# First GNN layer: one PSUM bank for small results in two halves, and a block's end with three steps between its hops

## The chip, the cores and the metric

The kernel runs on one core of a Trainium2 chip. The metric is device time in microseconds. The kernel before has a median of 3425.99 us over three runs (3420.14 to 3426.87).

A core has five engines that run their own instruction streams and wait for each other by semaphores: TensorE (PE: matrix products and transposes, with PEld its weight loads), VectorE (DVE), ScalarE (ACT), GpSimd (POOL, which here issues the gathers) and SyncE (SP, which issues DMAs; ScalarE issues some too). TensorE writes to PSUM, and VectorE or ScalarE read the results from there.

## The reference, cut to what matters

The whole computes two rounds of a graph layer and an expert layer on 6250 nodes of 256 values. The change is in the first graph layer:

```python
def _L0_gnn_ref(x, edge_index, edge_attr, u, batch, W1, b1, W2, b2):
    row, col = (edge_index[0], edge_index[1])
    h = jnp.concatenate([x[row], edge_attr], axis=1)
    h = jax.nn.relu(h @ W1 + b1)
    agg = jax.ops.segment_sum(h, col, num_segments=N_NODES)
    cnt = jax.ops.segment_sum(jnp.ones((h.shape[0],), h.dtype), col, num_segments=N_NODES)
    agg = agg / jnp.maximum(cnt, 1.0)[:, None]
    out = jnp.concatenate([x, agg], axis=1)
    return jax.nn.relu(out @ W2 + b2)
...
x = x + _L0_gnn_ref(_layernorm(x, axis=-1), edge_index, edge_attr_256, ...)
x = x + _L0_ffn_ref(_layernorm(x, axis=-1)[None], ...)[0]
```

There are 106250 edges, sorted by their destination `col`. The expert layer that follows begins with a normalization of x and a product with W_gat; both are already made here, at the end of each block of nodes.

## The kernel before, in words

**Tiling.** The nodes lie in 49 windows of 128 (a block's end, in the change's words, is a window's end). The edges of a window are worked on in three groups, so there are 147 groups, numbered q. A group has six tiles of 128 edges.

**One group.** `load_sources` gathers the rows of the sources (six indirect DMAs by POOL) into one of four ring buffers h. `load_attr` loads the edges' attributes in eight DMAs, four issued by SyncE and four by ScalarE (L1410). `turn` transposes them on VectorE (L1500). `hidden(q, j)` multiplies two of the six tiles by the lower half of W1 into PSUM (ph, L1115, 8 records in the trace each time). `join` adds the gathered rows on VectorE (L1518), and a relu follows on ScalarE (L1519). `add_up` sums the edges of equal destination on TensorE, by matrices of zeros and ones that `equal` made (pe, L1541).

**The order.** It is written out by hand: `Ordered.pin` keeps each engine's instructions in program order through the main loop (L1632 to L1656). An iteration q has join(q-1), hidden(q, 0), add_up(q-2), the gathers of q+2, turn(q+1), hidden(q, 2), equal(q), hidden(q, 4), and at last new attribute loads. Generators are advanced at three places between, by `steps`. This text calls them slots:

- A, between hidden(q, 0) and add_up: a step of the sorting for a later stage (VectorE), then one step of each window's end that is under way;
- B, between hidden(q, 2) and hidden(q, 4): one step of each window's end;
- C, after hidden(q, 4): a step of `windows` (which prepares the indices of later windows), then one step of each window's end.

**A window's end** (`end_of`, L1547) starts after its last add_up, in slot B. It is a chain of hops between engines: divide by the count (ag, ScalarE L1554); transpose (TensorE L1109, into pt) and copy out (gt, ScalarE L1110); four products with W2 (pm, L1115, a pt tile too); bias, relu, residual and statistics of x on VectorE (L1566 to L1575) and a square root on ScalarE (L1576); the normalized x (xn, ScalarE L1582); transpose and copy out to b_all (the same lines); two products with the W_gat columns (pg, L1115, pt again), and three copies on ScalarE (L1593 to L1595). A `yield` ends a step. With A1 for slot A of the group after the one in which the end started, the steps lie at B0, A1, C1, A2, B2, A3, C3, ten steps in all. One group has three, and a window ends every nine steps.

**The PSUM tile pt.** [...] one buffer of one bank, for everything that is small. A pt tile is 128 x 256 float32[...]. The next tile of the pool waits until the last one has been read. Besides a window's end, `find_starts` (L1034) and `load_windows` (L1152) use it in slot C, for six blocks of seven windows each, during the first 100 groups; and `sorted_edges` (L1332) at the end of the layer.

**The window loads.** `load_windows` also lets SyncE issue 14 small loads, raw_src and raw_dst (L1146), once per block. ScalarE's attribute loads [...] wait for those before them.

## Time and profile before

The profile is of one execution, which took 4171.77 us; its span, from the first to the last instruction, is 4169.9 us. The runs without a profile took 3426 us. So a duration taken from the profile is compared with the profile's own total.

| row of the page | busy us | mean ns |
|---|---|---|
| ph<-w1b,et, TensorE, x3528 | 869.1 | 399 |
| pe<-h,eq, TensorE, x3168 | 256.9 | 397 |
| h<-y_dram,src, POOL gathers, x882 | 850.7 | 965 |
| h<-ph,h, VectorE join, x147 | 258.2 | 1756 |
| h<-h, ScalarE relu, x147 | 218.2 | 1484 |
| et<-ea, VectorE turn, x147 | 260.8 | 1774 |

| small work of the windows' ends (trace, in the first layer) | mean ns |
|---|---|
| pt<-ident,o (transpose, 2 records of a kind each time) | 287 |
| pt<-w,b_all and pt<-w,o (pm, 8 records) | 391, 400 |
| pt<-wgx,b_all (pg, 4 records) | 260 |
| o<-pt and b_all<-pt, ScalarE copies | 368 |
| o<-pt,b; x_all<-o,x_all; ln_st<-x_all, VectorE | 417, 425, 427 |
| o<-x_all,off,ln_rs, ScalarE | 600 |

How to read it: a line of the page names line, engine, operation, what is written and read, and how often; then busy time, the mean of one, and the idle time of the engine just before, with what ended it. TensorE's records overlap, so the mean of one is longer than what one adds. A float32 product is two records. The granted TensorE clock was 0.856 of full speed over the span, and 0.93 in the first layer.

### The profile page before, as it was taken

Reading aid. Unit: us, or ns where it says so; the run is one execution under the profiler, and the core shown is the slowest. Engines: PE = TensorE matmul, PEld = TensorE weight load, DVE = VectorE, ACT = ScalarE, POOL = GpSimd, SP = SyncE. Lnnn points to the kernel's source line nnn. Section 1 sums busy time; section 2 is a strip of 40 time slices with the busy share of each in tenths; the row PEclk is TensorE's granted clock in tenths of the full one; section 3 lists DMA queues with packets and bytes.
Section 4 is the critical chain, followed back from the end, with each engine's and each line's share of the span. In section 5 each row is a group of like instructions: output and inputs, shape, how many; then the busy total and the mean of one; then the engine's idle time right before and its main releaser. Section 6 shows DMA issues by size and latency. Waiting matters only on the chain.

```text
span 4169.9 us, 57220 instructions
## 1 busy us (share of the span) xinstructions
PE 3317.5 (80%) x18509; PEld 2590.9 (62%) x18509; DVE 2154.3 (52%) x5685; ACT 1125.4 (27%) x2014; POOL 2256.1 (54%) x2364
## 2 busy tenths in 40 slices
PE   7787889888889985888898888785356766867788
PEld 5566666666666664677787777673234544555566
DVE  5565666665555653656455657564223333433344
ACT  4122222222222222324435344452011211111123
POOL 0555566566666635455454545524666666665651
PEclk8899999999999997999999999896567777776678
DMA  6676767777777732323333334233111111111110
GB/s 192 156 166 152 169 160 173 170 166 165 171 168 176 167 99 54 78 66 95 82 84 99 92 88 114 73 79 96 45 45 52 50 50 50 51 51 48 52 49 21
DMA packets 698912, 428.56 MB, mean 103 GB/s; under 512 B 531272, under 2 KB 640315, under 8 KB 698604
## 3 DMA queue, kind: packets, MB, share of 16 engines
q0 software_dynamic: 89408, 178.08, 18.3%
q1 hardware_dynamic: 365948, 187.21, 16.9%
q10 hardware_dynamic: 243248, 59.52, 7.2%
q8 instruction: 150, 2.46, 0.3%
q14 instruction: 158, 1.29, 0.1%
HBM read 382.05 MB, written 42.49 MB: 102 GB/s over the span
## 4 chain that ended last, share of the span: by engine, by line
PE 47%; another core or an unknown queue 10%; issue 10%; DVE 7%; POOL 5%; ACT 3%; DMA 2%; SPq 1%; DVEq 0%; ACTq 0%; POOLq 0%
PE ph L1115 21%; PE py L1115 10%; PE pe L2524 4%; POOL hg L1128 4%; PE pt L1115 3%; PE po L1884 3%; PE pe L1541 3%; POOL h L1128 1%; PE pa L1821 1%; DMA rb<-low_dram 1%; PE pt L1109 1%; ACT hh L1720 1%; ACT L1720 1%; DVE eq L2503 1%
## 5 line engine op out<-in xcount | busy, mean ns | idle before, releaser
L1128 POOL DMA_INDIRECT h<-y_dram,src x882 | 850.7, 965 | 645.5 <-issue 511.0
L1128 POOL DMA_INDIRECT hg<-hp_dram,src x831 | 786.9, 947 | 460.9 <-issue 230.8
L1128 POOL DMA_INDIRECT sg<-gat_dram,src x640 | 613.4, 958 | 613.3 <-DVE px L1856 334.0
L1115 PE MATMUL ph<-w1b,et 128*128 128x256 f32 x3528 | 869.1, 399 | 28.6 <-issue 22.1
L1115 PEld LDWEIGHTS ph<-w1b,et 128*128 128x128 f32 x3528 | 681.9, 198 | 196.8 <-issue 104.9
L2524 PE MATMUL pe<-eq,hg 128*128 128x96 f32 (+15 forms) x2036 | 376.5, 334 | 150.6 <-issue 90.4
L2524 PEld LDWEIGHTS pe<-eq,hg 128*128 128x128 f32 x2036 | 361.3, 252 | 214.6 <-issue 147.9
L1115 PE MATMUL py<-w,hh 128*128 128x256 f32 x1568 | 415.3, 404 | 77.2 <-ACT hh L1720 34.6
L1518 DVE TENSOR_TENSOR h<-ph,h 128x1536 f32<-128x1536 f32 x147 | 258.2, 1756 | 371.7 <-remote 164.3
L1519 ACT ACTIVATE h<-h 128x1536 f32<-128x1536 f32 x147 | 218.2, 1484 | 762.5 <-DMA ea<-in_edge_attr_dram 284.1
L2503 DVE TENSOR_SCALAR eq<-px,dst,ew 128x96 f32<-128x96 f32 x831 | 261.4, 367 | 312.2 <-remote 117.1
L1115 PE MATMUL ph<-b_all,w 128*128 128x256 f32 (+1 forms) x1600 | 411.4, 397 | 10.5 <-issue 10.3
L1115 PEld LDWEIGHTS py<-w,hh 128*128 128x128 f32 x1568 | 302.4, 201 | 130.3 <-ACT hh L1720 40.8
L1115 PEld LDWEIGHTS ph<-b_all,w 128*128 128x128 f32 x1600 | 304.6, 200 | 53.5 <-issue 16.5
L1541 PE MATMUL pe<-h,eq 128*32 128x257 f32 x3168 | 256.9, 397 | 68.1 <-issue 63.2
L1884 PE MATMUL po<-pp,B 128*128 128x240 f32 (+10 forms) x1280 | 261.8, 345 | 10.2 <-issue 8.4
L1500 DVE STREAM_TRANSPOSE et<-ea 128x1536 f32<-128x1536 f32 x147 | 260.8, 1774 | 14.8 <-issue 7.8
L1720 ACT ACTIVATE hh<-ph,b 128x256 f32<-128x256 f32 (+1 forms) x400 | 165.5, 467 | 360.9 <-remote 127.2
L1884 PEld LDWEIGHTS po<-pp,B 128*128 128x128 f32 x1280 | 222.3, 195 | 25.0 <-issue 9.7
L1541 PEld LDWEIGHTS pe<-h,eq 128*32 128x32 f32 x3168 | 104.1, 112 | 177.6 <-issue 124.9
L1115 PE MATMUL py<-ew,g 65*128 65x256 f32 x392 | 140.7, 485 | 49.8 <-DVE x_all L2479 33.5
L1863 DVE TENSOR_TENSOR pp<-px,A 128x960 f32<-128x960 f32 (+10 forms) x160 | 156.0, 975 | 42.1 <-remote 26.0
(339 smaller groups left out, 3825.0 us busy)
## 6 DMA issues: line engine op xcount, KB each, us to landing
ea<-in_edge_attr_dram SPq DMA_DIRECT2D x588, 96.0 KB
ea<-in_edge_attr_dram ACTq DMA_DIRECT2D x588, 96.0 KB
y<-y SPq DMA_DIRECT2D x196, 128.0 KB
w<-in_L_ffn_W_dram SPq DMA_DIRECT2D x48, 512.0 KB
y<-ys SPq DMA_DIRECT2D x96, 256.0 KB
rb<-low_dram SPq DMA_DIRECT2D x80, 256.0 KB
h<-y_dram,src POOLq DMA_INDIRECT x882
hg<-hp_dram,src POOLq DMA_INDIRECT x831
```

The source lines that it names most:

```text
L1109: TE.transpose(pt[:, c, :], src[:, c * P : (c + 1) * P], ident)
L1115: TE.matmul(dst, lhs(c), rhs(c), start=c == 0, stop=c == n - 1)
L1128: GP.indirect_dma_start(out=dst, out_offset=None, in_=table[0:NP, :], in_offset=IndirectOffsetOnAxis(ap=idx, axis=0),)
L1500: V.transpose(et[q].rearrange("p c m k -> p m c k"), ahead.pop(q).rearrange("p i m (c k) -> p (i m) c k", c=2),)
L1518: V.tensor_add(h, ph.pop(q), h)
L1519: SC.activation(h, h, AF.Relu)
L1541: TE.matmul(sums[w][b * Q : (b + 1) * Q, :], eq[k][:, j, at], h[:, i * NT + j, 0:WS], start=g == 0 and j == NT - 1, stop=g == last_of[b] a ...
L1720: SC.activation(hidden[u][:, f, :n, :], ph[:, f - f0, :n, :], AF.Gelu, bias=b1[:, e, f : f + 1],)
L1863: V.tensor_tensor(pps[g, half][:, :, 0:n, :], pay[:, js, :].unsqueeze(2).to_broadcast([P, HG, n, HV]), near[g][:, js, 0:n].unsqueeze(3).to ...
L1884: TE.matmul(po.rearrange("p b v -> p (b v)"), B[:, j, :], pp[:, j, 0:n, :].rearrange("p b v -> p (b v)"), start=half == 0 and j == 0, stop ...
L2503: V.tensor_scalar(equals[k][:, j, :], lanes[:, 0:NW], dst_of[:, t : t + 1], ew[:, t : t + 1], op0=OP.is_equal, op1=OP.mult,)
L2524: TE.matmul(sums[b][:, lo - t0 * P : hi - t0 * P], hg[:, j, :], eq[:, j, lo - n0 : hi - n0], start=False, stop=after >= (t0 + n) * P,)
```

## The change

A class `Halves` takes the whole bank as one tile and hands out its two halves in turn. In `end_of` four places that had two yields get three, so that a window's end has fourteen steps, and the steps lie at B0, B1, B2, C2, A3, A4, A5. Ends of two windows then overlap by five steps instead of one. In `sorted_edges` the tile's shape is cut to what a half holds.

```diff
+class Halves:
+
+    def __init__(self, pool, width):
+        self.width, self.last = width, 1
+        self.bank = pool.tile([P, 2, width], F32, name="pt")
+
+    def tile(self, shape, dtype, name):
+        n = math.prod(shape[1:])
+        assert dtype == F32 and n <= 2 * self.width
+        if n > self.width:
+            v = self.bank.rearrange("p a k -> p (a k)")[:, 0:n]
+        else:
+            self.last = 1 - self.last
+            v = self.bank[:, self.last, 0:n]
+        return v if len(shape) == 2 else v.rearrange("p (c k) -> p c k", c=shape[1])
...
-                pt = pst.tile([P, 4, P], F32, name="pt")
+                pt = pst.tile([P, 2, P], F32, name="pt")
...
-                tc.tile_pool(name="p1", bufs=1, space=PSUM) as psm,
+                tc.tile_pool(name="p1", bufs=1, space=PSUM) as pends,
...
+                psm = Halves(pends, D)
...
                     SC.activation(ag, pe[:, 0:D], AF.Copy, scale=rc)
-                    yield
-                    yield
+                    for _ in range(3):
+                        yield
                     gt = wk.tile([P, D], F32, name="o")
                     transposed(psm, gt, ag)
-                    yield
-                    yield
+                    for _ in range(3):
+                        yield
                     pm = psm.tile([P, D], F32, name="pt")
...
                     SC.activation(xn, x_all[:, w, :], AF.Identity, bias=off, scale=rs)
-                    yield
-                    yield
+                    for _ in range(3):
+                        yield
                     transposed(psm, b_all[:, w, :], xn)
-                    yield
-                    yield
+                    for _ in range(3):
+                        yield
                     pg = psm.tile([P, D], F32, name="pt")
```

More of the change, by code (lines that the diff above doesn't have):

```diff
@@ L1 @@
+import math
 from contextlib import ExitStack
```

## The prediction

> **What bounds the kernel now.** I read the page first, for the share of each engine and its slices.

> ```profile
> span 4169.9 us, 57220 instructions
> ...
> PE 3317.5 (80%) x18509; PEld 2590.9 (62%) x18509; DVE 2154.3 (52%) x5685; ACT 1125.4 (27%) x2014; POOL 2256.1 (54%) x2364
> ```

> Then the table of stretches, for the first layer alone (joins run from 107.7 to 1512.8 us):

> ```profile
> 150.00:1000.00 850.00, 736.08 (x4534) 549.48 (x4533) 525.98 (x1024) 191.87 (x321) 507.34 (x528) 0.93 0.74 165
> 1000.00:1500.00 500.00, 448.51 (x2736) 332.54 (x2736) 285.18 (x478) 116.34 (x196) 308.95 (x318) 0.93 0.73 166
> ```

> The first column of times is the stretch, then PE, PEld, DVE, ACT, POOL busy. PE is at 87% and 90%, no other engine over 62%. So the layer is TensorE's, and only what TensorE waits for counts. Third, TensorE's order of time over one whole window of three groups:

> ```profile
> 1309.17 0.38 PE L1109 MATMUL pt<-ident,o 128*128 128x128 f32 x2
> 1309.48 1.51 PE L1541 MATMUL pe<-h,eq 128*32 128x257 f32 x24
> 1310.92 3.72 PE L1115 MATMUL ph<-w1b,et 128*128 128x256 f32 x16
> 1314.47 1.03 PE L1115 MATMUL pt<-w,b_all 128*128 128x256 f32 x4
> 1315.34 1.03 PE L1115 MATMUL pt<-w,o 128*128 128x256 f32 x4
> 1316.20 1.89 PE L1115 MATMUL ph<-w1b,et 128*128 128x256 f32 x8
> ...
> 1332.21 0.38 PE L1109 MATMUL pt<-ident,o 128*128 128x128 f32 x2
> ```

> From one first transpose (1309.17) to the next (1332.21) it is 23.04 us without a gap: nothing to win here. POOL's 18 gathers, 0.95 us each and 0.30 between, need 22.5 us in the same time, so it is next in line. Last, what TensorE waited for in the earlier stretch, where the window loads run beside:

> ```profile
> PE pt L1115 <- DVE dst L1170: 20.9, 3, 10.5
> ...
> PE pt L1109 <- DVE ix_g L1164: 10.6, 2, 10.3
> PE pt L1115 <- DVE start L1036: 10.4, 2, 10.0
> PE pt L1115 <- ACT h L1519: 5.2, 3, 4.1
> ...
> PE pt L1115 <- ACT b_all L1110: 2.9, 1, 2.9
> ```

> The columns are us in all, times, longest. All rows with pt add up to 73 us. But four waits of about 10 us (41 us) lie where DVE, ACT and PE all stand and only POOL goes on. Such holes come about every 56 us also where no pt is near (DVE idle 10.83 us before 1357.83), so these four are not pt's to give back. Some 32 us are left: (a) pm or pg behind VectorE's reading of a window tile in the same slot C: 0.4 to 2.3 us, six clean ones, mean 0.8; (b) the first transpose behind the readers of the last pg: 4.0, 2.0, 2.0, 0.5, 0.3, together 8.8; (c) ScalarE held up by the loads of raw_src and raw_dst: 4.1, 3.9, 2.9, 1.3, 1.2, 0.8, together 14.2; (d) others, 1.9.

> **Part 1, the halves.** They add no instruction. What they allow depends on whether a write to one half may run while the other is read. No trace shows it, since the pool had one buffer, whose next tile always waited for the last reader. [...] The built program has it so: a first transpose into one half waits for the ScalarE copy out of the other, and pm for the three pg copies. By address, every wait of kinds a to d would go (9 + 8.8 + 14.2 + 1.9, less 3 for VectorE below): -31 us. By bank the hand-overs stay, and their distance decides. I take the bank. What the halves do give is that pm may lie unread while a window tile uses the other half.

> **Part 2, the steps.** With a group's slots A, B, C, a window ends thus, before: B0 ag, A1 first transpose, C1 pm, A2 normalize, B2 xn, A3 second transpose, C3 pg. After: B0, B1, B2, C2, A3, A4, A5. The same instructions run; the order changes.

> *Gone.* C holds no pm or pg any more. Of 18 uses of pt by windows (6 blocks, 3 each) 11 stood before a pm or pg by their group numbers, at 0.8: -9 us. The first transpose no longer follows pg by one slot: -8.8. Kind d: -1.9. Together **-20 us**. What is late next is POOL, 0.55 us a window behind, 27 us over 49 windows, so this gain would fit.

> *New: two hand-overs one slot apart.* Second transpose (A4) and the next window's first (B4) share a group; so do pg (A5) and the next pm (B5). Within a group join starts some 0.2 us after the first matmul, 1.76, then ScalarE's relu 1.48: it ends at 3.5, or near 4.1 where the four ea issues (2.2 us) come first. The copy (0.37) is done at 4.5; slot B comes at 1.8 + 0.3 + 1.4 + 1.8 = 5.3. So 0.8 us of slack, and about as much for pg's three copies (0.5). Before, the same copies had until C, 1.8 us more. No cost in a quiet window. Where relu is late, it is paid. Of the groups with that transpose, eleven had a relu later than that by 0.1 to 2.8 us without window loads, 8 us together; of those with pm's B, about 1: **+9 us**.

> *The window loads.* Six times the four ea issues on ScalarE wait for loads that SyncE spreads over 10 us, and relu stands behind them (ScalarE's order of time, then TensorE's):

> ```profile
> 740.51 1.48 ACT L1519 ACTIVATE h<-h 128x1536 f32<-128x1536 f32 x1 [3.63 <-DMA h<-y_dram,src]
> ...
> 748.09 5.01 ACTq L1410 DMA_DIRECT2D ea<-in_edge_attr_dram  x4
> 753.38 1.48 ACT L1519 ACTIVATE h<-h 128x1536 f32<-128x1536 f32 x1 [11.11 <-DMA ea<-in_edge_attr_dram]
> ```

> ```profile
> 756.11 0.44 PE L1109 MATMUL pt<-ident,o 128*128 128x128 f32 x2 [1.33 <-issue]
> ```

> The group begins at 746.08 and its relu ends at 754.86, 8.8 later; TensorE paid only 1.33, at the next transpose. After, pm (1.73) leaves the C before this group and stands in its B: the relu ends at 10.5 by the group's own start, the copies at 11.0, slot B is at 5.6: a wait of 5.4. The same for the others, by group: q9 5.3, q24 2.7, q38 8.4, q52 none (its B holds nothing), q80 6.4. Sum 28 against 14.2: **+14 us**. Those of q38 and q80 overlap a hole and may be smaller.

> *VectorE at C2.* Normalize (0.42, 0.42, 0.43, 0.18, 0.15, with gaps 1.74) moves from A2 to C2, ahead of join and its PSUM buffer. pm ends one pair of hidden (1.8 us) before the group does, so the chain is hidden by that pair. Where a window tile is read at C2 too (7 times) the pair is used up; join is then 2.7 us late, the transpose of the group after it 0.4: **+3 us**. Without the pair it would be 1.7 x 49 = 85 us.

> *ScalarE and its queue.* The Sqrt comes before the four ea issues of that group, which start about 3 us later; they are needed three groups (23 us) on. Costs nothing; uncovered, 3 us a window. SyncE's and POOL's queues are not passed. The write of gat_dram comes a few slots later, once in seven windows, with no reader before the layer ends. At the end of the layer the last window takes the same chain, with six more expert matmuls (0.43 each) before its pg and one reload of ScalarE's table (1.28) fewer: bounds -2 to +3. I take **+2**, since TensorE is nearer to being the bound there (gaps of 0.4 to 1.3 us from 1527 to 1546) than ScalarE.

> **Sum**: -20 + 9 + 14 + 3 + 2 = +8, by the profiled execution 4171.8 + 8 = 4180 (its span 4169.9 and 1.9 around it). The runs shown have a median of 3425.99, 18% less. The holes, 10 us in 56, have the same share, but no run shows that they are missing there. I carry the 8 us over whole: **3434 us**, +0.23%.

> **Rivals.**
> 1. *The gain is left alone.* Relu's lateness is partly the holes' doing; without them the window loads cost what they did (0 net) and the late ones nothing: -20 + 3 = -17, 3409. For it: q38 and q80 overlap holes. Against: q66 has none, and SyncE takes 1.5 us a pair of loads there.
> 2. *The slack of 0.8 us is not there* (slower): the copy waits for more than its transpose. The row for it: a second transpose ends at 1269.4, its copy starts at 1271.16 with ScalarE free since 1270.76, 0.4 late. From a shortfall of 0.4 on in both hand-overs, 49 x 2 x 0.4 = +39 us: 3465. Against: the three pg copies came 0.04 us after pg.
> 3. *Nothing is moved.* POOL, 0.55 us a window behind, sets the pace once TensorE has fewer gaps, and late relus are made good in its slack: 3426.

> **How the numbers follow.** Forecast 0.5, rival 1 0.25, rival 2 0.15, rival 3 0.1. From no change a measurement tells about 0.2%, 7 us. The forecast's own span is 3424 to 3445, so of its 0.5, 0.32 is slower, 0.15 the same, 0.03 faster; rival 1 gives 0.22 faster, 0.03 same; rival 2 slower; rival 3 0.07 same, 0.03 slower. Slower 0.5, same 0.25, faster 0.25. The range goes from rival 1 to most of rival 2: 3408 to 3460.

> **What would show it.** Right: no pm or pg in slot C; TensorE's waits for DVE dst, start and ix_g down to holes; waits before pt<-ident,o and pt<-w,b_all on ACT b_all and a_dst of 3 to 8 us at five of the six window loads. Wrong: quiet windows other than 23.0 us (rival 2 if longer); those five waits missing (rival 1); a transpose into one half that runs beside a copy of the other[...].

## The result and the profile after

The changed kernel is slower: 3451.68 us, median of five runs (3448.12 to 3462.11), against 3422.96 (3418.70 to 3426.87) on the same chip. The ratio is 1.0077, with a 95% interval of 1.0063 to 1.0092: +28.7 us, where +8 was forecast.

The head of the page of the changed kernel, and the same lines of a second profile of the kernel before (run b0 below), which is needed because the first profile, of 4170 us, was stretched by holes (stretches of some 10 us in which VectorE, ScalarE and TensorE all stand) that the profiles at 3409 to 3455 us don't have:

```profile
span 3453.0 us, 57273 instructions
...
PE 3170.7 (92%) x18509; PEld 2538.7 (74%) x18509; DVE 2153.4 (62%) x5685; ACT 1120.6 (32%) x2013; POOL 2250.7 (65%) x2364
```

```profile
span 3416.2 us, 57220 instructions
...
PE 3164.1 (93%) x18509; PEld 2531.4 (74%) x18509; DVE 2155.8 (63%) x5685; ACT 1126.9 (33%) x2014; POOL 2251.2 (66%) x2364
```

The busy times agree within 7 us: no work was added. The span grew by 37. Where it grew, a table of stretches shows, from the first hidden of group 3 to that of group 146; before, then after (stretch, PE, PEld, DVE, ACT, POOL busy, granted clock, DMA share, GB/s):

```profile
119.60:1234.90 1115.30, 1103.43 (x7353) 856.22 (x7352) 822.96 (x1520) 311.33 (x517) 826.90 (x861) 1.00 1.00 203
```

```profile
121.70:1264.50 1142.80, 1110.03 (x7348) 864.70 (x7348) 822.63 (x1520) 306.60 (x516) 828.26 (x861) 0.99 0.95 198
```

The same groups take 27.5 us longer. TensorE is busy for 6.6 us more with the same instructions, at a granted clock of 0.99 instead of 1.00, and idle for 20.9 us more (32.8 against 11.9). What it waits for in these stretches is in the table of waits; the rows in which TensorE waits on pt for another engine, before and then after (us in all, times, longest):

```profile
PE pt L1115 <- ACT o L1110: 3.9, 2, 2.1
...
PE pt L1109 <- ACT o L1582: 2.8, 3, 1.3
PE pt L1115 <- DVE ix_g L1164: 2.1, 3, 0.7
...
PE pt L1115 <- DVE dst L1170: 1.5, 4, 0.4
PE pt L1115 <- DVE start L1036: 1.0, 4, 0.3
```

```profile
PE pt L1127 <- ACT b_all L1128: 18.5, 5, 7.7
...
PE pt L1133 <- ACT a_dst L1614: 11.8, 3, 4.1
```

Two things are to be seen. The waits behind window tiles (DVE ix_g, dst, start) are gone, as forecast, but there were only 4.6 us of them. And the two new hand-overs, first transpose behind the second (b_all) and pm behind pg (a_dst), hold TensorE for 30 us.

How one of them comes about, at group 80: ScalarE's order of time, then TensorE's.

```profile
752.67 5.50 ACTq L1428 DMA_DIRECT2D ea<-in_edge_attr_dram  x4
758.45 1.48 ACT L1538 ACTIVATE h<-h 128x1536 f32<-128x1536 f32 x1 [9.53 <-DMA ea<-in_edge_attr_dram]
759.84 0.36 ACT L1128 ACTIVATE b_all<-pt 128x256 f32<-128x256 f32 x1
```

```profile
749.44 0.38 PE L1127 MATMUL pt<-ident,o 128*128 128x128 f32 x2
...
760.25 0.69 PE L1127 MATMUL pt<-ident,o 128*128 128x128 f32 x2 [7.07 <-ACT b_all L1128]
760.74 6.37 PE L1133 MATMUL ph<-w1b,et 128*128 128x256 f32 x16
```

The four attribute loads hold ScalarE until 758.2 (5.50 us for their issue, 2.33 for that of the next four), relu follows, and only then the copy of the second transpose, which had been in PSUM since 749.8. TensorE stands for 7.07 us. And it is not back at speed afterwards: the 16 records of ph take 6.37 us, 3.62 in a quiet window. The stretches after two of the long waits and after one of 2 us show the granted clock:

```profile
176.00:184.00 8.00, 8.00 (x42) 5.82 (x41) 5.12 (x12) 2.10 (x3) 6.12 (x7) 0.80 1.11 214
...
760.20:768.20 8.00, 7.95 (x38) 6.41 (x42) 3.80 (x4) 2.07 (x6) 0.00 (x0) 0.62 0.93 152
...
538.30:546.30 8.00, 8.00 (x57) 6.53 (x58) 4.89 (x8) 2.07 (x5) 5.90 (x7) 1.00 1.19 220
```

After one wait of 3.90 us the clock is 0.80, after 7.07 us 0.62, after 2.03 us 1.00. The length alone does not set it: after the other wait of 3.9 us it is 0.68, after that of 7.7 us 0.69. What does is told in the last section.

### The profile page after: what moved, and what is told of

It reads as the page before. It is cut to its first block, busy times and chain, and to the rows that moved or that the text cites. A ratio compares the mean times of both kernels' runs of the same rounds, so it can differ in the third digit from the quotient of the medians.

```text
span 3453.0 us, 57273 instructions
## 1 busy us (share of the span) xinstructions
PE 3170.7 (92%) x18509; PEld 2538.7 (74%) x18509; DVE 2153.4 (62%) x5685; ACT 1120.6 (32%) x2013; POOL 2250.7 (65%) x2364
## 4 chain that ended last, share of the span: by engine, by line
PE 59%; POOL 14%; DMA 11%; issue 7%; DVE 5%; ACT 2%; SPq 1%; ACTq 0%; DVEq 0%; POOLq 0%
PE ph L1133 30%; POOL hg L1146 14%; PE py L1133 10%; DMA hg<-hp_dram,src 6%; PE po L1903 5%; PE pe L1560 5%; PE pt L1133 3%; DMA ea<-in_edge_attr_dram 2%; DMA rb<-low_dram 1%; PE pe L2543 1%; PE pa L1840 1%; PE pt L1127 1%; DVE et L1519 1%; PE pm L1133 1%; DVE x_all L2084 1%
## 5 line engine op out<-in xcount | busy, mean ns | idle before, releaser
L1133 PE MATMUL ph<-w1b,et 128*128 128x256 f32 x3528 | 831.6, 388 | 12.3 <-DVE et L1519 9.8
L1133 PEld LDWEIGHTS ph<-w1b,et 128*128 128x128 f32 x3528 | 661.2, 192 | 159.0 <-issue 70.7
L2543 PE MATMUL pe<-eq,hg 128*128 128x96 f32 (+15 forms) x2036 | 435.0, 349 | 161.3 <-DMA hg<-hp_dram,src 128.3
L2543 PEld LDWEIGHTS pe<-eq,hg 128*128 128x128 f32 x2036 | 380.9, 255 | 266.0 <-issue 97.8
L1133 PE MATMUL py<-w,hh 128*128 128x256 f32 x1568 | 387.4, 387 | 5.9 <-ACT hh L1739 5.4
L1133 PE MATMUL ph<-b_all,w 128*128 128x256 f32 (+1 forms) x1600 | 385.4, 380 | 2.9 <-issue 2.8
L1133 PEld LDWEIGHTS py<-w,hh 128*128 128x128 f32 x1568 | 291.5, 192 | 43.3 <-ACT hh L1739 7.7
L1133 PEld LDWEIGHTS ph<-b_all,w 128*128 128x128 f32 x1600 | 290.1, 190 | 35.6 <-issue 3.2
L1519 DVE STREAM_TRANSPOSE et<-ea 128x1536 f32<-128x1536 f32 x147 | 260.8, 1774 | 16.2 <-DMA ea<-in_edge_attr_dram 10.6
L1903 PE MATMUL po<-pp,B 128*128 128x240 f32 (+10 forms) x1280 | 252.2, 337 | 2.7 <-DVE acc L1909 2.5
L1560 PE MATMUL pe<-h,eq 128*32 128x257 f32 x3168 | 217.7, 385 | 0.0
```

Source lines behind the costliest of these rows:

```text
L1133: TE.matmul(dst, lhs(c), rhs(c), start=c == 0, stop=c == n - 1)
L1519: V.transpose(et[q].rearrange("p c m k -> p m c k"), ahead.pop(q).rearrange("p i m (c k) -> p (i m) c k", c=2),)
L1560: TE.matmul(sums[w][b * Q : (b + 1) * Q, :], eq[k][:, j, at], h[:, i * NT + j, 0:WS], start=g == 0 and j == NT - 1, stop=g == last_of[b] a ...
L1903: TE.matmul(po.rearrange("p b v -> p (b v)"), B[:, j, :], pp[:, j, 0:n, :].rearrange("p b v -> p (b v)"), start=half == 0 and j == 0, stop ...
L2543: TE.matmul(sums[b][:, lo - t0 * P : hi - t0 * P], hg[:, j, :], eq[:, j, lo - n0 : hi - n0], start=False, stop=after >= (t0 + n) * P,)
```

## Experiments

The theory (L): the window loads' hold of ScalarE is the cost, and most of the gain that was counted did not exist. The rival (G): the gain is there, and something else costs more. All ratios are to the kernel before on the same chip. Four kernels were first compared on a chip on which the kernel before takes 4238 us; they ran again, under names ending in _2, on chips like the first, and these runs are told first. The other chip comes at the end of the section.

**b0: the kernel before, profiled again.**

```diff
-                work, sort, slow = [], [sorting()], [windows()]
+                work = []
+                sort, slow = [sorting()], [windows()]
```

> The kernel before with one line split in two, which changes no instruction: a second profile of it, since the first was stretched by holes of 10 us that the profile of the changed kernel doesn't have. Theory L (the window loads are the whole difference: the 20 us of waits that were counted as gone were the holes' doing or are hidden, and the changed kernel's five waits behind the held ScalarE, 3.9, 3.9, 7.7, 4.1 and 7.1 us, together 26.6, are nearly all new): in a profile without holes, TensorE's waits for pt in the first layer add up to less than 8 us, and the layer's joins end some 25 to 30 us earlier than the changed kernel's. Rival G (the gain of some 20 us is there, and a larger loss lies elsewhere): the waits for pt add up to 20 us or more, the first layer is at most 12 us shorter than in the changed kernel, and the rest of the 29 us lies behind it.

It took 3418.09 us (one run). The rows with pt above add up to 11.3 us, between the two expectations: 4.6 behind window tiles, 6.1 behind the held relu (single gaps of 1.3, 2.1, 0.9 and 1.8) and small ones. The main loop is 27.5 us shorter than the changed kernel's, as L says. Of the waits of the first transpose behind pg's readers (8.8 us in the first profile) there are none. I also measured each window from trace times of the first hidden of its three groups. The six windows (three groups each) with the loads (from groups 9, 24, 36, 51, 66, 78) take 146.6 us here and 178.4 after, +31.8; the other 41 take 954.5 and 948.6, -5.9. So L: the loss lies in six windows.

**halves and steps: each part alone.** In halves the four loops are two yields again. In steps the pool has its one buffer, and slot C is turned round:

```diff
-                psm = Halves(pends, D)
...
-                    steps(slow)
+                    steps()
+                    for some in list(slow):
+                        if next(some, slow) is slow:
+                            slow.remove(some)
```

> The halves alone, with two steps between the hops as before. [...] both theories expect no change: ratio 1.000, within 0.002. A rival, that the halves may be used independently, expects the waits of pm and pg behind window tiles to go: 9 us less by the prediction's count, ratio 0.997 or lower, if those waits are there without the holes.

> The three steps alone, with one buffer of the bank as before; so that pm can be read before a window tile takes the buffer, the windows' step stands behind the ends' step in slot C. If the halves do nothing but let pm lie unread, this is as slow as the whole change: ratio 1.006 to 1.010. If the halves' bookkeeping costs something by itself, it is faster than the whole change by over 7 us, ratio below 1.006.

halves: 1.0002 (0.9990 to 1.0013). In the traces no write to one half lies beside a read of the other: in the changed kernel's, from 100 to 1300 us, none of the 307 reads of pt by ScalarE and VectorE overlaps a write of it by TensorE, and the write after a read starts 0.05 us or more behind the read's end. steps: 1.0081 (1.0059 to 1.0104), the whole change's loss. Halves are needed only so that pm may lie unread while a window tile passes; the lost time comes from the steps.

**after_spread: the loads thinned out.**

```diff
                     SY.dma_start(v[at : at + CW, :], rows)
-            for _ in range(3):
                 yield
+            yield
+            yield
```

> The changed kernel with the 14 small loads of a block spread over seven groups, one pair a group, where all were issued in one. Nothing else is moved but the block's later steps, by six groups. ScalarE's attribute loads then wait for one pair at most (some 1.5 us). Theory L: the five waits of 4 to 8 us before pt<-ident,o and pt<-w,b_all are gone and with them nearly all of the loss: 3452 - 26 = 3426, ratio 1.000, within 0.003. Rival G expects the same gain of 26 us here, since the waits are there in both; it is told apart by b0. If the waits go and the time stays above 1.005, they were not what the change cost.

0.9967 (0.9959 to 0.9976), at the better edge of what was expected: 1.0077 - 0.9967 is 37.7 us. The rows of its table of waits, over the same groups:

```profile
PE pt L1127 <- ACT b_all L1128: 5.9, 5, 2.5
...
PE pt L1133 <- ACT a_dst L1615: 1.8, 1, 1.8
```

From 30.3 us to 7.7, and no wait is left that takes the clock down (1.00 over the loop). The six windows that had the loads take 138.1 us in its profile, 178.4 with the loads in one group. The five long waits with what they do to the clock were the loss.

**before_spread: the same edit on the kernel before.** Run a second time as before_spread_2 on a chip at 3430.74 us (the first time is at the end).

> The same kernel as before_spread, once more, since the first comparison fell on the chip at 4238 us. On a chip at 3426: without the four waits of b0 (6.1 us) 3420, ratio 0.998. At 0.998 or above the halves and the three steps are worth some 4 us once the loads hold nobody (after_spread had 0.9967); at 0.9967 or below they are worth nothing there either.

0.9951 (0.9939 to 0.9964), 3412.56 us: better than expected, and not above the changed kernel with spread loads (0.9967, whose interval just meets this one). The loads cost the kernel before 0.0049 or 17 us, not 6; b0 was one run, with mild loads (halves, with the same hops, has a wait of 5.32 us at the group where b0 has 2.07). With the loads out of the way the change is worth nothing.

**steps_spread: slot C turned round, spread loads, one buffer.** As steps and after_spread together; run a second time as steps_spread_2, on the same chip as before_spread_2.

> The same kernel as steps_spread, once more, for the same reason. On a chip at 3426: ratio 0.9945 if the window tiles ahead of normalize cost after_spread its 8 us, 0.9967 if the order in slot C is worth nothing.

0.9943 (0.9931 to 0.9954), 3409.65 us: as expected, 8 us below after_spread. The windows that begin at groups 18, 39, 60, 99 and 120 and have a tile in C2 are 23.1 to 23.2 us long here, 24.1 to 25.1 in after_spread, 7 us together. So the tile ahead of normalize, on VectorE, cost 7 to 8 us. From before_spread_2 it can't be told (0.0008, intervals overlap).

**t2c: no two hand-overs behind one relu.**

```diff
                     SC.activation(xn, x_all[:, w, :], AF.Identity, bias=off, scale=rs)
-                    for _ in range(3):
-                        yield
+                    yield
+                    yield
                     transposed(psm, b_all[:, w, :], xn)
```

Run a second time as t2c_2, on a chip at 3428.58 us.

> The same kernel as t2c, once more: its first comparison fell on a chip on which the kernel before takes 4238 us, with holes in its first layer, and the whole change was not run there. On a chip where the kernel before takes 3426: the hand-over theory expects ratio 1.002 (0.999 to 1.005), with waits behind ScalarE of about 11 us in the load groups, none in slot order 0; the rival, that a hold costs the same wherever the hops lie, 1.0077.

1.0051 (1.0036 to 1.0065): between, on the edge of the theory's span, and not the rival's. In the load windows the theory holds: long waits only at groups 38, 52 and 80 (3.14, 4.11 and 3.94 us; at most 3.8 was said), and none over 0.8 where there had been three of 3.9 to 4.1. The six load windows take 159.0 us against 178.4: -19, where -24 was expected, because these three waits too were followed by a lower clock (1.7 to 3.3 us each; 0.58 and 0.79 granted in the 8 us after those of groups 38 and 80). And the other 41 take 961.4, 12.7 more where 5 was expected: first transposes that stand after a window tile in C (waits of 1.68, 1.97 and 1.64 us) among them.

**after_sp: the four held issues given to SyncE.**

```diff
-                        (SY if c < 2 else SC).dma_start(
+                        (SY if c < 2 or fresh else SC).dma_start(
```

Here fresh is set where the small loads are issued and cleared at the end of that group. Run a second time as after_sp_2, beside t2c_2.

> The same kernel as after_sp, once more, for the same reason. On a chip where the kernel before takes 3426: 0.997 to 1.001 if ScalarE's hold is the cost, 1.0077 if spreading helped in another way.

1.0049 (1.0034 to 1.0063): below the 1.0077 of the rival, but the 0.997 to 1.001 of the theory was missed. ScalarE is free in the group after the loads, and held one group later, where its next four issues take as long:

```profile
408.18 5.68 ACTq L1431 DMA_DIRECT2D ea<-in_edge_attr_dram  x4
414.14 1.48 ACT L1542 ACTIVATE h<-h 128x1536 f32<-128x1536 f32 x1 [11.18 <-DMA h<-y_dram,src]
```

TensorE then waits 6.22 us before pm (and 5.57 at group 81), less at the other loads (2.4 and below, 2.6 at group 53). The hold was moved, not taken away, and the long waits moved with it; what was gained, 10 us, goes with the waits that became short.

**The same four kernels on another chip.** There the kernel before takes 4238.28 us, and the first layer moves 151 to 175 GB/s, not 184 to 209 (rows by slice of t2c and of the changed kernel).

> The kernel before with its small loads spread in the same way, so that the change can be weighed where no loads hold ScalarE. In b0 TensorE waited 1.3, 2.1, 0.9 and 1.8 us behind the held relu, 6.1 us together; without them 3426 - 6 = 3420, ratio 0.998. The changed kernel with spread loads had 0.9967. If this one is at 0.998 or above, the halves and the three steps are worth some 4 us of gain once the loads are out of the way (the quiet window is 22.96 us with them and 23.05 without, 0.09 x 49 = 4.4); if it is at 0.9967 or below, they are worth nothing.

> The changed kernel with the small loads in one group as they were; only the attribute loads that follow them in the same group go all eight to SyncE, so that ScalarE issues none there and is not held. The windows' steps stay where they are. If it is ScalarE's hold that costs, the waits of 4 to 8 us before pt<-ident,o and pt<-w,b_all are at most 1 us each and the time falls by 20 to 30 us: ratio 0.997 to 1.001. If after_spread was faster because the windows' steps lie elsewhere or the transfers are thinner, this stays near 1.0077.

> Three steps with one buffer, the ends' step ahead of the windows' step in slot C, and spread loads. In after_spread the windows with a window tile in C2, ahead of normalize on VectorE, were longer than 22.96 us by 1.1, 2.1, 2.2, 1.1 and 1.6, 8 us together. If that is VectorE's order there, they go: 3415 - 8 = 3407, ratio 0.9945. If the halves are needed, that is, if the tile behind normalize costs TensorE as much as normalize behind the tile did, the ratio stays at 0.9967.

> The changed kernel with two steps instead of three between xn and the second transpose: that lies in C3 and pg in C4, so that no two uses of pt by ends follow each other within one group behind the same relu. Loads as in the changed kernel. Theory (a hold is paid where a hand-over has its copy behind the held relu): the groups held in slot order 0 (three of the six) pay nothing, the others at most 3.8 us: the waits behind ScalarE fall from 26.6 to about 11 us, the slow stretches after them from about 10 to 2, against some 5 us of second transposes and pg's behind window tiles in C: 3452 - 19 = 3433, ratio 1.002 (0.999 to 1.005). Rival (a hold of ScalarE costs what it costs wherever the hops lie): 1.0077 again.

before_spread 1.0007 (0.9989 to 1.0024), after_sp 0.9999 (0.9977 to 1.0022), steps_spread 0.9988 (0.9971 to 1.0005), t2c 0.9953 (0.9935 to 0.9970). In all of their profiles TensorE stands for 150 us and more in the loop. t2c, with after_sp the slowest of the four on the other chips, is the best here, and of what spreading the loads gave little or nothing is left. Why, the runs don't settle; the whole change was not run on that chip either.

## Why the prediction was right, and where it was off

It said slower, by the window loads, and that is what happened; 3451.68 lies in its range (3408 to 3460), but beyond the forecast's own span of 3424 to 3445. The mechanism is right, most sizes are not, and that its sum came out above nothing is in part luck: two terms were too large by 15 and 9 us, with opposite signs, and without the second of them the sum would have been -1. By the terms of its sum:

- **Halves wait like one buffer: right.** halves alone 1.0002. Before the result it was shown by the built program alone; the trace of the changed kernel has it at group 80, where the transpose into one half starts 0.05 us after the copy out of the other ends (759.84 + 0.36, then 760.25).
- **Quiet windows: right.** 22.96 us after, 23.05 before; the 0.09 (4 us over the layer) was not foreseen. This ends rival 2, the missing slack of 0.8 us. Rival 3, in which POOL's pace makes late relus good, ends with the waits of 28.6 us below, which were paid in full.
- **Gone waits, -20: too large, about -5.** The four waits of 10 us were rightly left out, but most of the rest was not there either in a profile without holes: 4.6 us stood behind window tiles (9 forecast), none behind pg's readers (8.8), none of kind d (1.9). The step that failed is taking waits of 0.3 to 4 us out of a disturbed execution as its undisturbed part.
- **Late relus, +9: too large, 1 to 2.** Outside the groups of the window loads the two new hand-overs cost 1.7 us in the changed kernel's loop, and 0.7 us in the whole loop of steps_spread_2. (In after_spread they cost 7.7 us, 5.0 of it at groups 47 to 50 behind issues of ScalarE that took 3.5 and 3.8 us, so that is a hold again.) The lateness went with the holes, as rival 1 said of it; so this error and the last partly cancel.
- **Window loads, waits of 28: right in place and size.** Forecast, by group: q9 5.3, q24 2.7, q38 8.4, q52 none, q66 5.4, q80 6.4. Measured: 3.9, 3.9, 7.7, 2.0 (q53), 4.1, 7.1, together 28.6. Rival 1, in which they shrink with the holes, falls. The 14.2 before stand against 16.8 by the medians, and 6 in b0's single profile.
- **The same term, net +14: mis-sized, +21** (37.7 - 16.8). What it lacked is the clock. Measured from the end of each wait to the start of the group after next, against a quiet window, TensorE lost 1.8, 2.6, 2.5, 1.8 and 3.0 us after the five waits from 3.9 us up, 11.7 together, and 0.1 after those of 1.2 and 2.0. The trace grants half the clock for one, two, three, one and three stretches of 3.41 us; half of what of them lies behind each wait is 1.7, 2.6, 2.5, 1.7 and 3.0 us, which is the loss. The sum has no term for it.
- **Normalize at C2, +3: mis-sized, 7 to 8** (after_spread less steps_spread_2). The join is late as forecast (2.9 us after the group's start at groups 13, 28 and 70, 0.2 to 0.5 in quiet groups), but what waits is not the next user of join's PSUM buffer. In VectorE's program order turn of the next group stands behind join and is late with it, and the first weight load of that next group's hidden loads what turn makes (et). Behind the joins of groups 13, 28 and 70 it starts 0.1 us after turn ends and 2.9 to 3.4 us after join ended, having waited 0.9, 1.3 and 1.0 us (VectorE, then the weight loads, at group 13; the row names the engine's last work before, not what it waited for):

```profile
205.98 1.76 DVE L1537 TENSOR_TENSOR h<-ph,h 128x1536 f32<-128x1536 f32 x1
208.75 1.78 DVE L1519 STREAM_TRANSPOSE et<-ea 128x1536 f32<-128x1536 f32 x1 [0.21 <-DMA ea<-in_edge_attr_dram]
```

```profile
210.65 1.59 PEld L1133 LDWEIGHTS ph<-w1b,et 128*128 128x128 f32 x8 [0.85 <-PE pt L1171]
```

The rest of this term is paid at first transposes of later groups (1.25 us at group 44, 0.42 at 86).
- **Tail, +2: near.** From hidden of group 146 to the first expert product with w and hh 38.8 us, 35.3 in b0: +3.5.

Together the runs give +21 (loads), +8 (order in slot C) and -3 (all the rest: steps_spread_2 less before_spread_2, forecast -9): +26, where 0.0077 is 26.4. They must agree, since each term is a difference of two of the same ratios. A run outside the sum does not fit it: steps has the better order in slot C with the loads in place, so it should lie 8 us below the whole change, at 1.0053; it measured 1.0081 (1.0059 to 1.0104). In the one profile of each, the loop of steps is 11.2 us shorter than the changed kernel's (1131.5 against 1142.7). So what the order in C is worth beside the loads stays open.

## What to carry to other kernels

When results are handed on closer together, look for what can delay the engine that frees the buffer, and price it at its worst case, not its quiet one: here the slack of 0.8 us held in every quiet window, and five holds of ScalarE in the layer ate it. Where an engine issues DMAs between its computations, look at how long these issues take: here ScalarE's relu at group 80 stood behind four of them that took 5.50 us. Thin out the burst first (one edit, 17 us on the kernel before); moving some of the issues to another engine moved the wait in after_sp (5.68 us, one group later). And a wait of TensorE cost more than itself where the clock went down: here it did after every one of 3.1 us and more, and after one of 2.35 us (1.8 to 3.0 us on top of the five of 3.9 to 7.7 in the changed kernel).

## What was not expected of the hardware

```profile
183.84:187.25 3.41, 1.06 (x6) 0.85 (x6) 3.12 (x7) 2.14 (x3) 2.51 (x3) 1.00 1.21 219
187.25:190.67 3.42, 3.42 (x10) 2.70 (x9) 0.41 (x1) 0.00 (x0) 2.79 (x3) 0.50 1.17 232
...
525.17:528.58 3.41, 2.31 (x16) 1.44 (x8) 1.56 (x3) 0.32 (x1) 2.50 (x4) 1.00 1.27 218
528.58:531.99 3.41, 1.92 (x10) 1.74 (x11) 0.00 (x0) 1.82 (x3) 2.80 (x3) 1.00 1.20 211
```

TensorE was idle for 2.35 us of the first stretch, and for 1.10 and 1.49 us of the last two. In the loops of the nine profiles at 3409 to 3455 us all 17 stretches at full clock with 2.01 us of idle time or more were followed by half clock, and none with 1.97 us or less. (On the other chip the two mix between 1.6 and 2.0 us; so they do in the first profile of the kernel before, half clock after 1.60 and 1.93 us, full clock after 1.72.) So in these nine profiles 2.01 us in one stretch was enough, a wait of 2.0 us or less was not followed by half clock, and between 2.0 and about 4 us (twice 2.0, spread evenly over two stretches; an estimate from these numbers) it depends on where in the stretches the wait falls.

- Two chips 24% apart on the same kernel (3426 and 4238 us), with different orders of the same variants. The first profile of the kernel before, with 152 to 176 GB/s in the layer, looks like the second chip's, and its holes with it; what makes them is not settled.
